# Four-row strips, later turns and a re-queued last layer in a two-layer attention and window-product kernel

## Chip, cores and metric

One core of one Trainium2 chip. The metric is device time of one execution in microseconds (us). The core has five engines that run their own instruction streams in order: TensorE (PE; its weight loads are listed as PEld), VectorE (DVE), ScalarE (ACT), GpSimd (POOL) and SyncE (SP). DMAs are issued by SyncE, ScalarE or GpSimd; what one engine has issued forms a queue of its own. In the profile q1 is SyncE's queue, q10 ScalarE's, and q0 (software_dynamic) GpSimd's.

## The reference, cut to what matters

The input x is one image of 48 channels, 256 x 256, in float32.

```python
# layer 0: x = x + L0(group_norm(x)), 16 groups
qkv = einsum('bchw,oc->bohw', xn, w_qkv)      # 48 -> 144 channels
qkv = dwconv3x3(qkv, w_dw)                     # depthwise, padding 1
q, k, v = (heads(unfold(t)) for t in split(qkv, 3))
# unfold: patches of 4x4 pixels, with a border of 4 zero pixels; 8 heads of 96 elements
attn = softmax(einsum('bhcn,bhcm->bhnm', l2norm(q), l2norm(k)) * temperature)
out = fold(einsum('bhcn,bhnm->bhcm', v, attn))
x = x + einsum('bchw,oc->bohw', out, w_proj)
# layer 1: x = x + L1(group_norm(x)); windows of 64x64 pixels
out = einsum('bcphqw,twW,thH,tcC->bCpHqW', xb, Ws, Hs, Cs)   # t = 3 terms
```

There are 4096 patches per head, so attention is 8 products of 4096 x 4096, with 96 elements per patch.

## The kernel before

The work runs in stages, and nearly all of the time is in the third.

**Start (0 to about 285 us).** Group sums of x, then the pointwise product to q, k and v for heads 0 and 1 (L154), written to a DRAM tensor t1[0]. The depthwise convolution of head 0 (class Depthwise, `depthwise_first`) follows; its patches go to DRAM as qkv[0].

**Attention (to about 3180 us).** For each of 8 heads h there are 16 groups g of 256 query rows; in each group two blocks of 128 rows. `scores` (L570) makes a block's 128 x 4096 scores in four PSUM tiles of the pool "big" (three buffers; matmuls at L344), and ScalarE takes their exponentials (L580). `weigh` (L606) multiplies the group's exponentials with the values (L614, three PSUM tiles of the same pool per group), and VectorE adds the result to an accumulator (L628). The order of every engine's instructions is the order in which the program text issues them (`tc.manual_schedule`). One group is written as: loads of values and keys, scores of two blocks, turns of values, then four steps k = 0 to 3, the first three with a `weigh` each.

Into this order the rest of layer 0 is woven:

- *Depthwise of the next head* (class Depthwise, L195): in groups 0 to 11 of heads 0 to 6, a row-block r is loaded in group r-1 (SyncE), gets its nine taps (VectorE, L232) in the next, and two groups after r is scaled, rearranged into patches (ScalarE, L286), split into a high and a low part (ScalarE L292, GpSimd L296) and stored from GpSimd (L302): the value patches as soon as they are there, the low part and both other stores at k=0. The low part's buffer is shared with the squares (L243) that VectorE reduces at L247.
- *Strips* (class Strip, L166): the pointwise product for heads 2 to 7 is made during head 0. A strip is two rows in each half of the image. Its steps are load (xs, SyncE L175), run (two matmuls at L181 into a "big" tile, then ScalarE's copy with bias into one of three buffers ot, L184) and store to t1[1] (two DMAs, SyncE L193). At steps k=1 and k=3 of each group two strips are run and two are loaded; at k=2 and at k=0 of the next group these two are stored. All 64 strips are done within head 0.
- *Values* (`load_value` L553, `turn` L559): a block of 512 values is loaded (vt, two buffers) and transposed on TensorE (L562) into vT (nine buffers). In head 0 the blocks 2 to 7 are loaded at the start of groups 1 to 6 and turned later in the same group. For the next head all eight are loaded and turned in groups 11 to 14, two a group. Group g needs block g // 2.

**Projection (about 3180 to 3337 us).** The attention's output comes back from DRAM (pot, L789), is multiplied with the projection (L803) and added to x (L810), group sums are taken (L814), and the result x1 is stored to DRAM (L819). After the last sums the statistics of layer 1 are worked out on small tiles; between them `occupy` (L840) issues matmuls whose result nobody reads: seven in a row ahead of the statistics, then single ones, all on the tile nmx.

**Last layer (from 3337 us).** Eight units u (a row of windows yw and one half xh of the width). `over_c` (L911) multiplies rows of x1 (pieces lxq in SBUF) with Cs into PSUM tiles pa, and the copy into zt (L933 on ScalarE for one in four, L935 on VectorE) turns the layout from rows outermost to rows innermost in memory. `over_w` (L940) multiplies with Ws and ScalarE copies the result (lyt, L956), `over_h` (L961) multiplies with Hs, and `residual` (L977) adds x1 rows (lrt) and stores the output from GpSimd. Per unit there are three thirds q, each with three `over_w`; the steps of `over_c` for the next unit are woven between them, so that twelve steps of unit 0 stand alone at the beginning. Loads of later rows and pieces are kept in a list, and `begin_load` (L906) issues one of them at a time from ScalarE.

Of the kernel before, what the change touches and what calls it, by code (L numbers as in the profile page):

```python
# [17 lines left out]
C = 48  # L18
# [21 lines left out]
NOT = 3  # L40
# [6 lines left out]
def conv_preact_kernel(  # L47
# [118 lines left out]
    class Strip:  # L166
# [5 lines left out]
        def load(self):  # L172
            self.xs = cv.tile([64 + C, 2, W], F32, name="xs", bufs=3)
            for s, rows in enumerate(both_halves(xc, 2 * self.j, 2)):
                nc.sync.dma_start(out=self.xs[s * 64 : s * 64 + C], in_=rows)  # L175

        def run(self, ps):
            self.ot = ots[self.j % len(ots)]
            for s in range(2):
                r = slice(s * 64, s * 64 + C)  # L180
                nc.tensor.matmul(  # L181
                    ps[:M1, s, :], lhsT=wr[r], rhs=self.xs[r].rearrange("p a b -> p (a b)"), start=True, stop=True
                )
            nc.scalar.activation(  # L184
                self.ot[:, :, 1 : W + 1],
                ps[:M1].rearrange("p s (a b) -> p (s a) b", a=2),
                AF.Identity,
                bias=bias[:M1, 1:2],
            )
# [305 lines left out]

    ots = [cv.tile([M1, 4, W + 2], F32, name=f"ot{i}") for i in range(NOT)]
    for t in ots:
        nc.gpsimd.memset(t[:, :, 0:1], 0.0)
        nc.gpsimd.memset(t[:, :, W + 1 : W + 2], 0.0)
    depthwise_first()  # L500

    with tc.If(nc.values_load(large) > 0):
        with tc.tile_pool(name="sps", bufs=2, space=PSUM) as sps:
            for j in range(HALF // 2):
                w = Strip(j)
                w.load()
                w.run(sps.tile([128, 2, 512], F32, name="sps"))
                w.store()
# [27 lines left out]
    with tc.tile_pool(name="ahead", bufs=2) as ah, tc.tile_pool(name="ae", bufs=3) as ae, tc.tile_pool(  # L536
# [3 lines left out]
        NS = 3  # L540
        RP = TP // PX * KS
# [17 lines left out]
        def turn(h, m):  # L559
# [3 lines left out]
            vT = ah.tile([128, 4, HD], F32, name="vT", bufs=9)  # L563
# [89 lines left out]
        strips = [[Strip(s)] if s < HALF // 2 else [] for s in range(NH * NG * NK + 2)]  # L653
        for s in range(2):
            for w in strips[s]:
                w.load()
        with tc.manual_schedule():
            load_query(0, 1)
            block = scores(0, 0)
            for h in range(NH):  # L660
                more = h + 1 < NH
                rows = {r: Depthwise(h + 1, r) for r in range(CR + 1)} if more else {}
                for g in range(NG):
# [45 lines left out]
                    if h == 0 and 0 < g <= 6:  # L709
                        turn(0, g + 1)  # L710
                    if more and CR + 2 <= g < CR + 6:
                        for m in range(2):
                            turn(h + 1, (g - CR - 2) * 2 + m)
                    if p:
# [7 lines left out]
                    for k in range(NK):  # L722
# [10 lines left out]
                        if s % 2:  # L733
                            for w in strips[s - 1] + strips[s]:
                                w.run(big.tile([128, 2, 512], F32, name="big"))
                            for w in strips[s + 1] + strips[s + 2]:
                                w.load()
# [40 lines left out]
    with tc.tile_pool(name="pj", bufs=3) as pj, tc.tile_pool(name="pjs", bufs=1) as pjs, tc.tile_pool(  # L778
# [61 lines left out]
        def occupy(n):  # L840

            for _ in range(n):
                nc.tensor.matmul(busy[:, 0:2, :], lhsT=ident[:, :P2], rhs=nmx, start=True, stop=True)
# [219 lines left out]
```

## Time and profile before

| what | us |
|---|---|
| three runs | 3591.67, 3596.32, 3598.53 (median 3596.32) |
| the profiled execution itself | 3602.95 |
| its span, first to last instruction | 3601.1 |
| busy: PE | 3365.5 |
| busy: DVE | 2026.6 |
| busy: ACT | 1911.9 |
| busy: POOL | 523.9 |
| head 0, groups 2 to 15 | 346.75 to 754.2 |
| one later head (head 1) | 348.8 |
| last layer's first product to its last | 3337.2 to 3593.2 |

The mean granted TensorE clock is 0.972 of full speed. A row of the profile's timeline gives start, duration, engine, line, operation, output <- inputs and the number of instructions merged in it; in square brackets stands the idle time of the engine just before, and what ended it. In the groups of instructions a row gives count, busy time, mean ns of one, then the idle time before. A fp32 matmul is recorded as two passes, so counts of L614, L181, L923, L949 and L968 are twice those of the program text; those of L344 are not.

### The profile page before, as it was taken

What the parts mean: (1) busy time and instruction counts of PE and PEld (TensorE: products, weight loads), DVE (VectorE), ACT (ScalarE), POOL (GpSimd) and SP (SyncE); (2) the same over time, 40 slices, a digit from 0 to 9 for tenths busy, and PEclk for the clock granted to TensorE, in tenths of its full rate; (3) what the DMA queues carried; (4) which work ended last, traced back from release to release, by engine and by line L of the source; (5) the groups of instructions that cost most, each with busy time, mean ns of one, the idle gap of its engine ahead of it and who ended that gap; (6) DMA issues with size and microseconds to landing.
All of it is one profiled execution on the core that took longest, in us unless ns stands there. A gap on an engine that the chain in (4) does not pass through costs nothing.

```text
span 3601.1 us, 63050 instructions
## 1 busy us (share of the span) xinstructions
PE 3365.5 (93%) x25842; PEld 1871.5 (52%) x25842; DVE 2026.6 (56%) x2983; ACT 1911.9 (53%) x2890; POOL 523.9 (15%) x584
## 2 busy tenths in 40 slices
PE   2878898999999999999999999999999999976898
PEld 1334444555555555555555555555555555532675
DVE  5463665148825882587268727862885222258454
ACT  0245666557655665576456646764666444410443
POOL 2030111012211220122012211221121100010001
PEclk9999999999999999999999999999999999986899
DMA  7455655543332333233333323332233221059664
GB/s 156 165 114 158 156 156 143 166 129 92 87 86 84 97 81 89 83 92 86 82 86 97 91 80 83 94 90 81 80 96 93 64 57 37 19 121 289 140 158 108
DMA packets 240271, 384.10 MB, mean 107 GB/s; under 512 B 77618, under 2 KB 175266, under 8 KB 235464
## 3 DMA queue, kind: packets, MB, share of 16 engines
q1 hardware_dynamic: 187974, 244.77, 24.3%
q0 software_dynamic: 33728, 106.40, 13.1%
q10 hardware_dynamic: 18274, 28.83, 3.6%
q8 instruction: 206, 3.38, 0.4%
q14 instruction: 89, 0.73, 0.1%
HBM read 234.76 MB, written 144.90 MB: 105 GB/s over the span
## 4 chain that ended last, share of the span: by engine, by line
PE 81%; DMA 6%; DVE 2%; issue 1%; ACT 1%; SPq 1%; ACTq 0%; POOL 0%; POOLq 0%; DVEq 0%
PE big L344 38%; PE big L614 36%; PE pc L968 2%; PE pa L923 2%; PE pb L949 2%; DMA t<-ot 1%; PE big L181 1%; DMA pot<-os__70 1%; DMA vt<-qkv 1%; DMA lxq<-x1s 1%; DVE lzt L935 1%; DMA pad<-t 1%; PE pst L562 1%; DVE xt L810 1%; DMA x1s<-pxt 0%
## 5 line engine op out<-in xcount | busy, mean ns | idle before, releaser
L580 ACT ACTIVATE e<-big,nmx 128x1024 f32<-128x1024 f32 x1024 | 1144.3, 1118 | 902.8 <-PE big L344 886.9
L344 PE MATMUL big<-kt,qt 128*128 128x512 f32 x6144 | 1460.2, 395 | 35.1 <-DMA kt<-qkv 26.8
L614 PE MATMUL big<-e,vn 128*32 128x512 f32 x12288 | 1353.7, 595 | 1.0 <-DVE vn L598 1.0
L344 PEld LDWEIGHTS big<-kt,qt 128*128 128x128 f32 x6144 | 1142.6, 189 | 377.4 <-issue 120.1
L628 DVE TENSOR_TENSOR oacc<-big,oacc 128x1024 f32<-128x1024 f32 x359 | 438.6, 1222 | 784.2 <-PE big L614 784.2
L614 PEld LDWEIGHTS big<-e,vn 128*32 128x32 f32 x12288 | 385.2, 110 | 888.3 <-issue 818.1
L232 DVE SCALAR_TENSOR_TENSOR acc<-pad,dwt,acc 126x1024 f32<-126x1024 f32 x592 | 765.6, 1293 | 33.8 <-DMA pad<-t 13.4
L302 POOL DMA_DIRECT2D qkv<-o x72 | 53.1, 737 | 1349.0 <-ACT o L286 1349.0
L296 POOL TENSOR_TENSOR ol<-o,oh 126x1024 fp32r<-126x1024 f32 x78 | 185.2, 2375 | 277.3 <-DVE ss L247 204.4
L594 DVE TENSOR_REDUCE zt<-zs 128x1 f32<-128x5 f32 x256 | 38.7, 151 | 329.8 <-ACT e L580 329.8
L580 ACT ACTIVATION_READ_ACCUMULATOR e<-big,nmx 128x1 f32 x1024 | 196.4, 192 | 0.0
L286 ACT COPY o<-acc 126x1024 f32<-126x1024 f32 x74 | 160.7, 2172 | 0.0
L184 ACT ACTIVATE ot<-big,bias 108x1024 f32<-108x1024 f32 x64 | 68.9, 1112 | 136.7 <-PE big L181 71.0
L935 DVE COPY lzt<-pa 128x864 f32<-128x864 f32 (+1 forms) x69 | 102.1, 1525 | 63.5 <-PE pa L923 63.5
L956 ACT COPY lyt<-pb 128x1024 f32<-128x1024 f32 x69 | 70.9, 1028 | 112.6 <-PE pb L949 106.3
L803 PE MATMUL pps<-pot,wp 96*96 96x512 f32 x128 | 77.8, 773 | 53.3 <-DMA pot<-os__70 40.2
L213 ACT ACTIVATE acc<-pad,dwt 126x1024 f32<-126x1024 f32 x74 | 84.0, 1135 | 73.5 <-DMA pad<-t 73.5
L221 PE MATMUL dps<-pad,diag 126*126 126x512 f32 x216 | 96.4, 606 | 15.0 <-DMA pad<-t 15.0
L243 ACT ACTIVATE sq<-acc 126x1024 f32<-126x1024 f32 x74 | 78.4, 1060 | 59.8 <-DVE acc L232 48.9
L147 ACT ACT_TABLE_LOAD x2 | 2.6, 1283 | 202.6 <-DMA x1s<-pxt 149.2
L247 DVE TENSOR_REDUCE ss<-sq 126x64 f32<-126x1024 f32 x80 | 97.4, 1218 | 6.7 <-ACT sq L243 6.7
L949 PE MATMUL pb<-wsb,lzt 64*64 64x64 f32 x4608 | 88.8, 223 | 11.4 <-issue 7.2
(138 smaller groups left out, 1901.2 us busy)
## 6 DMA issues: line engine op xcount, KB each, us to landing
pad<-t SPq DMA_DIRECT2D x238, 254.0 KB
t<-ot SPq DMA_DIRECT2D x128, 217.7 KB
qkv<-ol POOLq DMA_DIRECT2D x78, 336.0 KB, 6.4
qkv<-oh POOLq DMA_DIRECT2D x70, 336.0 KB, 5.6
qt<-qkv SPq DMA_DIRECT2D x176, 96.0 KB
xs<-in_x_dram SPq DMA_DIRECT2D x128, 96.0 KB
pot<-os__70 SPq DMA_DIRECT2D x16, 768.0 KB
qkv<-o POOLq DMA_DIRECT2D x72, 168.0 KB, 3.4
```

What stands on the lines that cost most here:

```text
L213: nc.scalar.mul(self.acc, self.pad[:, 0:KS, 0:W], dwt[:, self.h, 0:1])
L221: nc.tensor.matmul(ps[:, i, :], lhsT=diag[:, tap, :], rhs=self.pad[:, y : y + 2, dx : dx + W], start=(tap == 0), stop=(tap == 8),)
L232: nc.vector.scalar_tensor_tensor(self.acc, self.pad[:, dy : dy + KS, dx : dx + W], dwt[:, self.h, tap : tap + 1], self.acc, ALU.mult, ALU.add,
L247: nc.vector.tensor_reduce(self.ss, self.sq.rearrange("p a (x b) -> p x a b", b=KS), AX.XY, ALU.add)
L286: nc.scalar.copy(self.o.rearrange("p (a b) x -> p a b x", a=KS), self.acc.rearrange("p a (x b) -> p a b x", b=KS))
L296: eng.tensor_sub(self.ol, self.o, self.oh.bitcast(F32))
L344: nc.tensor.matmul(ps[:, i, :], lhsT=qt[:, r, q0 : q0 + 128], rhs=kts[2 * j + i][:, r // 2, :], start=(r == 0), stop=(r == 2),)
L580: nc.scalar.activation(e[:, j * 1024 : (j + 1) * 1024], ps.rearrange("p a b -> p (a b)"), AF.Exp, bias=nmx[:, b : b + 1], accum_out=zs[:, ...
L614: nc.tensor.matmul(ps[p * 32 : (p + 1) * 32, u, :], lhsT=vn[:, c * 32 : (c + 1) * 32], rhs=e[:, n * 512 : (n + 1) * 512], start=(i == 0), ...
L628: nc.vector.tensor_add(oaccs[h, pair], ps, old)
L935: nc.vector.tensor_copy(to, src)
L949: nc.tensor.matmul(pb[s * WS : (s + 1) * WS, w, n * WS : (n + 1) * WS], lhsT=zts[u][r, t * C + b * 24 + q * 8 + s * 4 + i, :], rhs=wsb[r, ...
```

## The change

Four things are changed together.

1. Strips have four rows instead of two (`SR = 4`), so there are 32, with two buffers ot and two buffers xs of double size. One strip is run at k=1 and one at k=3, each in two parts of two matmuls and one copy; the next is loaded right after. The strip of k=1 is stored at k=2 and that of k=3 at k=0 of the next group, now from GpSimd, behind the depthwise's low part and stores at k=0.
2. Values: in head 0 the blocks 2 to 7 are loaded in groups 1, 2, 4, 5, 7 and 8 and turned two groups after that. For later heads seven blocks are loaded and turned in groups 11 to 14 of the head before, and the eighth is loaded in group 1 and turned in group 2 of its own head. vT has eight buffers.
3. Last layer: each load is issued from SyncE. Ahead of it SyncE issues a store of one element of the tile that was just copied, to a small DRAM tensor `turns`, so that the load is issued after that copy has been made. The copies of `over_c` keep input, output and engine but run with rows innermost.
4. The seven idle products ahead of the statistics become four, which read the last additions' result and the group sums.

```diff
-NOT = 3
+NOT = 2
+SR = 4
...
-            self.xs = cv.tile([64 + C, 2, W], F32, name="xs", bufs=3)
+            self.xs = cv.tile([64 + C, SR, W], F32, name="xs", bufs=2)
...
+            for i in range(0, SR, 2):
+                ps = pool.tile([128, 2, 512], F32, name="big")
...
+                nc.scalar.activation(
+                    self.ot[:, :, i : i + 2, 1 : W + 1],
...
         def store(self):
-            for s, rows in enumerate(both_halves(t1[1], 2 * self.j, 2, base=1)):
-                nc.sync.dma_start(out=rows, in_=self.ot[:, 2 * s : 2 * s + 2, :])
+            for s, rows in enumerate(both_halves(t1[1], SR * self.j, SR, base=1)):
+                nc.gpsimd.dma_start(out=rows, in_=self.ot[:, s])
...
-            vT = ah.tile([128, 4, HD], F32, name="vT", bufs=9)
+            vT = ah.tile([128, 4, HD], F32, name="vT", bufs=8)
...
+        LOADS = (1, 2, 4, 5, 7, 8)
...
-                    if h == 0 and 0 < g <= 6:
-                        load_value(0, g + 1)
+                    if h == 0 and g in LOADS:
+                        load_value(0, 2 + LOADS.index(g))
                     if more and CR + 2 <= g < CR + 6:
-                        for m in range(2):
+                        for m in range(2 if g < CR + 5 else 1):
                             load_value(h + 1, (g - CR - 2) * 2 + m)
+                    if h > 0 and g == 1:
+                        load_value(h, NM - 1)
...
-                    if h == 0 and 0 < g <= 6:
-                        turn(0, g + 1)
+                    if h == 0 and g - 2 in LOADS:
+                        turn(0, 2 + LOADS.index(g - 2))
...
+                    if h > 0 and g == 2:
+                        turn(h, NM - 1)
...
                         if k == 0 and p:
                             p.low(nc.gpsimd)
                             p.store((0, 1))
-                        if s % 2:
-                            for w in strips[s - 1] + strips[s]:
-                                w.run(big.tile([128, 2, 512], F32, name="big"))
-                            for w in strips[s + 1] + strips[s + 2]:
-                                w.load()
-                        elif s:
-                            for w in strips[s - 2] + strips[s - 1]:
-                                w.store()
+                        if s % 2 and s // 2 < len(strips):
+                            strips[s // 2].run(big)
+                            if s // 2 + 1 < len(strips):
+                                strips[s // 2 + 1].load()
+                        elif s % 2 == 0 and 0 < s // 2 <= len(strips):
+                            strips[s // 2 - 1].store()
...
-            occupy(7)
-            mv1, e1 = group_stats(st1, mean1, rstd1, pjs, pp1, lambda: occupy(1))
+            for ki in range(0, KS, 2):
+                occupy(xt[:, ys.start + ki : ys.stop : KS, :])
+            for i in range(0, 4, 2):
+                occupy(st1[:, : HALF * W // 512 - 3 + i, :])
+            mv1, e1 = group_stats(st1, mean1, rstd1, pjs, pp1, lambda: occupy(nmx))
...
-                        loads.append(lambda s=s, c=c: load_rows(yw, q, s, c, 4, nc.scalar))
+                        loads.append(lambda s=s, c=c: load_rows(yw, q, s, c, 4, nc.sync))
...
-        def begin_load():
-
-            if loads:
+        def begin_load(behind):
+
+            if loads and behind is not None:
+                n = len(taken)
+                taken.append(nc.sync.dma_start(out=turns[:, n : n + 1], in_=behind))
                 loads.pop(0)()
...
-                    if (p * 3 + g) % (4 if u else 2) == 1:
-                        nc.scalar.copy(to, src)
-                    else:
-                        nc.vector.tensor_copy(to, src)
+                    copy = nc.scalar.copy if (p * 3 + g) % (4 if u else 2) == 1 else nc.vector.tensor_copy
+                    copy(to.rearrange("p s y k -> p s k y"), src.rearrange("p s y k -> p s k y"))
...
-                    yield
+                    yield zt[0:1, 0, y : y + 1]
...
-                        begin_load()
+                        begin_load(parts[u, q][0:1, t, 0:1])
                         if t < 2:
                             for _ in range(2):
-                                next(ahead, None)
-                                begin_load()
+                                begin_load(next(ahead, None))
```

In the changed kernel the lines from L173 on are numbered some 1 to 15 higher.

More of the change, by code (lines that the diff above doesn't have):

```diff
@@ L494, in conv_preact_kernel @@
     one = attention.enter_context(tc.tile_pool(name="one", bufs=2, space=PSUM))
[L496 removed]
+    ots = [cv.tile([M1, 2, SR, W + 2], F32, name=f"ot{i}") for i in range(NOT)]
     for t in ots:
[L498 to L499 removed]
+        nc.gpsimd.memset(t[:, :, :, 0:1], 0.0)
+        nc.gpsimd.memset(t[:, :, :, W + 1 : W + 2], 0.0)
     depthwise_first()
@@ L503, in conv_preact_kernel @@
         with tc.tile_pool(name="sps", bufs=2, space=PSUM) as sps:
-            for j in range(HALF // 2):
+            for j in range(HALF // SR):
                 w = Strip(j)
                 w.load()
-                w.run(sps.tile([128, 2, 512], F32, name="sps"))
+                w.run(sps)
                 w.store()
@@ L647, in conv_preact_kernel @@
             turn(0, m)
-        strips = [[Strip(s)] if s < HALF // 2 else [] for s in range(NH * NG * NK + 2)]
-        for s in range(2):
-            for w in strips[s]:
-                w.load()
+        strips = [Strip(j) for j in range(HALF // SR)]
+        strips[0].load()
         with tc.manual_schedule():
@@ L889, in conv_preact_kernel @@
         loads = []
+        turns = dram.tile([1, 256], F32, name="turns")
+        taken = []
         def rows_later(yw, q):
```

43 lines of the change are left out of this document (23 added, 20 removed).

## The prediction

> **What bounds the kernel now.** I read the table of windows first, because the page's sums mix stages; then TensorE's timeline where the table shows it idle, then the engine named there. Columns of the windows: length, busy time of PE, PEld, DVE, ACT, POOL, granted clock, DMA share, GB/s.
>
> ```profile
> 346.75:647.60 300.85, 272.08 (x1643) 138.02 (x1641) 183.26 (x281) 191.01 (x262) 50.46 (x40) 0.95 0.58 152
> 647.60:754.20 106.60, 106.60 (x666) 56.62 (x665) 19.05 (x36) 58.83 (x94) 7.08 (x13) 0.97 0.58 170
> 754.20:1103.00 348.80, 348.80 (x2350) 196.39 (x2352) 219.91 (x341) 216.88 (x339) 57.75 (x53) 1.00 0.35 89
> 3337.00:3360.00 23.00, 19.20 (x153) 16.27 (x156) 8.72 (x6) 8.71 (x6) 0.00 (x0) 0.50 0.30 55
> 3360.00:3594.00 234.00, 214.06 (x6068) 160.50 (x6060) 125.92 (x90) 100.36 (x90) 19.55 (x28) 0.98 0.60 141
> ```
>
> Row 3 is head 1: PE is never idle, at full clock; the other heads look alike. Nothing that the change does there can show. Row 1 is groups 2 to 11 of head 0 (the strips run here): 29 us idle and a lower clock. Rows 4 and 5 are the last layer: its first 23 us run at half clock, then 20 us idle. Between head 7 and the last layer (3177 to 3337) the DMA share is near 1.0, and the change moves no transfer there. So the change can act in head 0 and in the last layer alone.
>
> What stops PE in head 0 (its timeline; in brackets the idle time before a row, and who ended it):
>
> ```profile
> 385.76 0.58 PE L562 MATMUL pst<-ident,vt 96*128 96x96 f32 x4 [3.11 <-DMA vt<-qkv]
> 386.26 8.77 PE L614 MATMUL big<-e,vn 128*32 128x512 f32 x64
> ...
> 406.98 8.50 PE L344 MATMUL big<-kt,qt 128*128 128x512 f32 x36 [1.40 <-ACT ot L184]
> ...
> 586.85 3.90 PE L181 MATMUL big<-xs,wr 48*108 48x512 f32 x8 [10.76 <-DMA xs<-in_x_dram]
> ```
>
> Three waits: a turn for a value block loaded in the same group, scores for ScalarE's copy into ot (itself waiting for an older store), strips for their load, late in SyncE's queue. Each costs twice: after 3.11 us idle the 64 products take 8.77 us and not 7.07. An undisturbed group lasts 25.75 us (scores from 528.06 to 553.81). Ten would be 257.5, with 2.3 us of turns 260; they took 300.85. **Excess 41 us**; in row 2 another 3 (a group at 647.6 that began cold). So 44 us is there to be had.
>
> **The change, part by part.**
>
> *Strips and turns: what goes.* The turns come two groups after their load; the wait of L562 (11.6 us, five times, on PE) goes. Loads and stores of a strip halve in number (128 to 64 each), and the stores leave SyncE's queue, so xs comes in time. In heads 1 to 7 one value block of eight is turned in group 2 of its own head, loaded a group earlier: no added wait, and head 1 has no idle time to give. I take all 44 us as removed.
>
> *Strips: the wait that is added.* There are two ot buffers instead of three. The strip of step k=3 writes the second one in each group; its store is issued at k=0 of the next group, and the buffer is written again at k=3 of that group. On POOL this store stands behind the patch store, the subtraction L296, and two 336 KB stores (L302), in groups 2 to 11. In the undisturbed group:
>
> ```profile
> 545.50 2.36 POOL L296 TENSOR_TENSOR ol<-o,oh 126x1024 fp32r<-126x1024 f32 x1 [3.29 <-DVE ss L247]
> 547.81 0.98 POOL L302 DMA_DIRECT2D qkv<-oh  x1
> 548.75 1.06 POOL L302 DMA_DIRECT2D qkv<-ol  x1
> ```
>
> and the queue's own rows (packets, MB, share; then count, KB, us from issue to landing, head 2's window):
>
> ```profile
> q0 software_dynamic: 33728, 106.40, 13.1%
> qkv<-ol POOLq DMA_DIRECT2D x10, 336.0 KB, 6.2
> ```
>
> Step by step: ol is issued at 548.75 and lands 6.2 us later, 554.95. Behind it come 2 x 435 KB. q0 moves 106.4 MB in 13.1% of 3601 us, 225 GB/s while it works, so 870 KB take 3.9 us: 558.85. Only then may ScalarE copy the strip (base: 551.45, 1.12 us each). Behind that copy on ScalarE stand the next exponentials; on PE the next scores, because strips and scores share three "big" buffers and the one needed is freed by that copy. So scores go on at 558.85 + 1.1 = 560.0, not at 553.81: 6.2 us. To it comes the cold start (after 4.34 us idle a row of 7.07 took 9.25): about 2. From it goes what VectorE gains in the idle time, since the sum before L296 ends earlier: about 1.5. I take **7 us** a group. Group 11 has no reduction ahead of L296 (in the trace it starts 4 us sooner): 3 us. 9 x 7 + 3 = **66 us**. Bounds: 3 us a group if the strip stores overlap the ol store to its last microsecond (30 us in all); above, the rows of ol in head 0 itself land after 11.2 us, but beside stores that leave SyncE, so I take 10 a group (93).
>
> The Trainium skill, "DMA: Bandwidth & Descriptors", section "Issuing engine by pattern", would have plain stores issued from SyncE. Its section on one DMA gives about 2 us plus bytes over 436 GB/s; the two stores by themselves would be an estimated 4 us, which leaves the place in the queue as the cost.
>
> Head 0 in all: 66 - 44 = **+22** (from -14 to +49).
>
> *Last layer, copies with rows innermost.* The copies write 4-byte pieces 256 bytes apart today. Rows by form:
>
> ```profile
> L935 DVE COPY lzt<-pa 128x864 f32<-128x864 f32 x46 | 77.4, 1707 | 48.0 <-PE pa L923 48.0
> L628 DVE TENSOR_TENSOR oacc<-big,oacc 128x1024 f32<-128x1024 f32 x359 | 438.6, 1222 | 784.2 <-PE big L614 784.2
> L286 ACT COPY o<-acc 126x1024 f32<-126x1024 f32 x74 | 160.7, 2172 | 0.0
> L286 ACT COPY o<-dps 126x1024 f32<-126x1024 f32 x6 | 6.1, 1012 | 13.6 <-DVE dps L281 10.3 <-issue 3.3
> ```
>
> 1707 ns for 864 elements against 1222 for 1024 contiguous ones: nearly double. L286 tells where strides cost: read from SBUF in steps of 16 bytes 2172, from PSUM 1012. So a write in runs of three (12 bytes) may cost 1.05 to 1.7 us; I take 1.2, nearest to L247, which reads runs of four at full rate (1218 for 1024). The read now steps 576 bytes through PSUM; no row shows VectorE doing that.
>
> The rule against it: "SBUF — State Buffer", section "Door 1: The DMA port swizzle", gives SBUF lines of 16 bytes, which agrees with the rows above, but PSUM lines of 8 bytes, outside of which access is slow for matmuls. If that held for these copies they would stay at 1.7 us, and with no gain from copies the sum at the end of this part would be +13 instead of +9.
>
> In the first 22 us of the layer (3337.2 to 3359.35) PE's own work at half clock is 8 x 1.89 + 4 x 1.36 = 20.6 us. With copies out of the way 1.5 us are saved; if unbroken work lets the clock rise as it did 6.5 us after 586.85, about 16 us remain and 6 are saved. I take -4.
>
> *Last layer, loads from SyncE.* Today they sit on ScalarE between its copies:
>
> ```profile
> 3529.62 3.47 ACTq L884 DMA_DIRECT2D lrt<-x1s  x2
> 3533.14 1.60 ACT L933 COPY lzt<-pa 128x864 f32<-128x864 f32 x1 [2.66 <-DMA lrt<-x1s]
> ```
>
> Two issues hold the copy for 2.66 us, and PE waits 1.96 behind it. Of the 20 us idle some 5 lie in the last 25 us, where no load is left. The steps that are long by PE's third product (10.6, 10.4, 11.2, 12.8 us against 9.1 to 9.5) add to 8. With shorter copies I take -9; bounds 0 and -17. The small stores on SyncE (88, one per load) wait for a copy's end; behind them only loads are queued, which the consumers need several steps later. SyncE has no other work here; an issue on it takes 0.3 to 0.6 us. If the loads came late for every second step, 1 us each would cost 12: upper bound +3 for the sum.
>
> *Idle products.* Before, 14 rows run from 3325.5 to 3330.5 in one go; now four, held back by the additions and sums they read, fill about the same time, beside VectorE's last additions, which set the end. Cost 0. If they kept the clock at 1.0 into 3337 they would save up to 8; if one came late, +1.
>
> Last layer in all: **-13** (from +4 to -25). Sum: +22 - 13 = **+9 us** on the profiled execution's own 3602.95 us (its span 3601.1). That run was 6.6 us above the median of the runs, so I put the change on the median: 3596.3 + 9 = **3605**.
>
> **Rivals.**
>
> 1. *Faster: the store lands early enough.* The point is 4.4 us a group: below it, head 0 gets shorter. At 3 us a group (30 in all) head 0 gains 14; with the 13 of the last layer the time is 3569. For: large packets, and SyncE's queue nearly empty of stores. Against: POOL's order puts them behind two stores that need 6.2 us even in head 2.
> 2. *The last layer gives little* (copies stay at 1.7 us, clock stays at half): -3, with the 22 of head 0, 3615. For: no row of such a read on VectorE, and the clock stayed at 0.5 at 83% busy. Against: L286 from PSUM.
> 3. *The store wait is larger*: 10 us a group, 93 in all, +49 - 13, 3632. For: ol lands after 11.2 us in head 0 today. Against: over a third of that traffic (8 x 218 KB of 152 GB/s x 30.1 us a group) was SyncE's own stores.
>
> **Chances.** A measurement of this kernel tells about 0.2% (7 us) from no change. Forecast 0.42 (3595 to 3615: 0.22 slower, 0.20 within), rival 1 0.36 (0.33 faster, 0.03 within), rival 2 0.13 and rival 3 0.09, both slower. Faster 0.33, within 0.2% 0.23, slower 0.44. Range: down to 3566 to take in most of rival 1, up to 3630 for half of rival 3.
>
> **What would show it.** In the profile after: POOL's stores t<-ot behind L302, ScalarE's copy into ot waiting for DMA t<-ot once a group in groups 2 to 11, PE idle 4 to 6 us after six score products, groups of about 32.5 us there and 25.8 in groups 12 to 15; no wait of pst for vt, none of strips for xs. In the last layer: lzt copies near 1.2 us on both engines, no DMA issue on ScalarE, a clock above 0.5 before 3355, PE idle below 12 us of the rest. Wrong if the ot copies do not wait (rival 1), or if the copies keep 1.7 us (rival 2).

## The result, and the profile after

The changed kernel takes **3652.4 us** (median of four runs, 3635.4 to 3658.8) against 3597.4 for the kernel before: ratio 1.0146, 95% interval 1.0108 to 1.0184, some 55 us slower. The forecast was 3605, its range ended at 3630. Single executions that ran far longer than all others of their kernel (6750 us in e4, 15546 in f4, one of 15132 of the kernel before) are slow runs and left out of every median and ratio here. The profiled execution took 3658.8 us, with a span of 3657.0 (before: 3601.1).

The table of windows after, cut as before: ten groups of head 0, the rest of head 0, head 1, the last layer's first steps, its rest to the last product. Columns as before: length, busy time of PE, PEld, DVE, ACT, POOL, granted clock, DMA share, GB/s.

```profile
346.69:700.78 354.09, 281.74 (x1654) 151.39 (x1652) 184.59 (x281) 191.37 (x264) 72.64 (x80) 0.89 0.48 128
700.78:805.30 104.52, 104.52 (x655) 54.88 (x656) 19.05 (x36) 57.73 (x93) 14.90 (x27) 0.98 0.56 161
805.30:1154.10 348.80, 348.80 (x2348) 196.45 (x2352) 219.81 (x340) 217.22 (x339) 59.92 (x58) 1.00 0.35 91
3397.00:3414.50 17.50, 14.82 (x132) 13.07 (x132) 5.91 (x6) 5.24 (x6) 0.00 (x0) 0.64 0.39 73
3414.50:3650.00 235.50, 214.09 (x6080) 162.90 (x6080) 94.17 (x90) 88.94 (x90) 19.50 (x28) 0.97 0.60 140
```

Row 1 is the loss: 354.1 us for ten groups that took 300.9. PE is idle for 72 us of them, and its clock fell from 0.95 to 0.89. Row 3 is head 1, unchanged to a tenth. Row 4 is shorter than before (17.5 against 22.1), row 5 is not. From the starts of the first score, the first score of head 1, the last score, the projection's first and last product and the last layer's first products, the 56 us of the two profiles are:

| stretch | before | after | difference |
|---|---|---|---|
| start to first score | 274.5 | 273.2 | -1.3 |
| head 0 | 459.8 | 512.1 | +52.3 |
| heads 1 to 7 | 2448.3 | 2448.8 | +0.5 |
| to the projection's first product | 27.7 | 28.3 | +0.6 |
| projection's products | 114.7 | 123.1 | +8.4 |
| statistics | 12.1 | 11.5 | -0.6 |
| last layer, first steps | 22.1 | 17.5 | -4.6 |
| last layer, rest to the end | 241.8 | 242.6 | +0.8 |

PE's timeline after, where it stood idle before it (three of ten such rows; the other seven are alike, 5.0 to 8.1 us):

```profile
485.00 12.28 PE L351 MATMUL big<-kt,qt 128*128 128x512 f32 x42 [8.12 <-ACT ot L191]
521.81 12.63 PE L351 MATMUL big<-kt,qt 128*128 128x512 f32 x42 [8.05 <-ACT ot L191]
559.37 12.61 PE L351 MATMUL big<-kt,qt 128*128 128x512 f32 x42 [8.45 <-ACT ot L191]
```

No wait for vt and none for xs is left in head 0. In their place stands one wait ahead of each group from 3 to 12, and 42 score products that took 9.80 us now take 11.4 to 12.6 behind it. What ends it, in the timeline of POOL and ACT in one group:

```profile
541.50 2.35 POOL L303 TENSOR_TENSOR ol<-o,oh 126x1024 fp32r<-126x1024 f32 x1 [2.30 <-DVE ss L254]
542.89 2.12 ACT L191 ACTIVATE ot<-big,bias 108x1024 f32<-108x1024 f32 x2 [1.69 <-PE big L184]
543.80 1.00 POOL L309 DMA_DIRECT2D qkv<-oh  x1
544.77 1.04 POOL L309 DMA_DIRECT2D qkv<-ol  x1
545.68 2.27 POOL L200 DMA_DIRECT2D t<-ot  x4
558.21 2.12 ACT L191 ACTIVATE ot<-big,bias 108x1024 f32<-108x1024 f32 x2 [13.19 <-DMA t<-ot]
```

POOL comes to the strip's store only at 545.68, when the strip of k=1 has been copied too, so all four stores leave at once. The copy of the strip of k=3 (last row) waits 13.2 us for the first two of them. The issues that start in this window (size of one, then us from issue to landing; SyncE's loads have none):

```profile
t<-ot POOLq DMA_DIRECT2D x4, 435.4 KB, 12.1
xs<-in_x_dram SPq DMA_DIRECT2D x2, 192.0 KB
qkv<-oh POOLq DMA_DIRECT2D x1, 336.0 KB, 7.0
qkv<-ol POOLq DMA_DIRECT2D x1, 336.0 KB, 11.0
vt<-qkv SPq DMA_DIRECT2D x1, 192.0 KB
```

The last layer's rest, groups of instructions from 3414 us on (busy, mean ns, then idle time before and who ended it):

```profile
L964 PE MATMUL pb<-wsb,lzt 64*64 64x64 f32 x4608 | 89.1, 223 | 14.0 <-issue 11.6 <-ACT lyt L971 1.6 <-ACT lzt L950 0.7
L983 PE MATMUL pc<-lyt,hsb 64*64 64x512 f32 x576 | 74.3, 626 | 6.8 <-issue 5.5 <-DVE lrt L997 1.3
L950 DVE COPY lzt<-pa 128x864 f32<-128x864 f32 (+1 forms) x63 | 61.5, 1002 | 56.0 <-PE pa L940 56.0
L950 ACT COPY lzt<-pa 128x864 f32<-128x864 f32 (+1 forms) x22 | 20.1, 914 | 13.0 <-PE pa L940 13.0
```

The same products in the kernel before, from 3359 us on:

```profile
L949 PE MATMUL pb<-wsb,lzt 64*64 64x64 f32 x4608 | 88.8, 223 | 11.4 <-issue 7.2 <-ACT lyt L956 2.4 <-ACT lzt L933 1.2
L923 PE MATMUL pa<-csn,lxq 49*128 49x144 f32 x896 | 70.7, 300 | 6.4 <-ACT lzt L933 2.6 <-DVE lzt L935 2.5 <-issue 0.9
L968 PE MATMUL pc<-lyt,hsb 64*64 64x512 f32 x576 | 70.3, 601 | 2.6 <-DVE lrt L982 1.3 <-issue 1.3
```

The copies are as fast as hoped: 1002 and 914 ns in the mean, 1531 and 1568 before. PE waits 2.3 us for the copies into lzt and lyt, where it waited 8.7. But its idle time put down to "issue", time for which the profile shows no releaser, is 17.6 us with the 0.5 of L940; before it was 9.4 in the same stretch. It lies inside runs of equal products whose inputs are all there. Below it is called idle time without a releaser.

### The profile page after: what moved, and what is told of

It is laid out like the page before. It is cut to its first block, busy times and chain, and to the rows that moved or that the text cites. A ratio compares the mean times of both kernels' runs of the same rounds, so it can differ in the third digit from the quotient of the medians.

```text
span 3657.0 us, 63059 instructions
## 1 busy us (share of the span) xinstructions
PE 3369.8 (92%) x25836; PEld 1882.6 (51%) x25836; DVE 1992.7 (54%) x2983; ACT 1896.7 (52%) x2890; POOL 558.5 (15%) x646
## 5 line engine op out<-in xcount | busy, mean ns | idle before, releaser
L351 PE MATMUL big<-kt,qt 128*128 128x512 f32 x6144 | 1477.8, 398 | 104.1 <-ACT ot L191 72.3
L351 PEld LDWEIGHTS big<-kt,qt 128*128 128x128 f32 x6144 | 1156.8, 191 | 449.4 <-issue 116.3
L303 POOL TENSOR_TENSOR ol<-o,oh 126x1024 fp32r<-126x1024 f32 x78 | 185.2, 2375 | 265.9 <-DVE ss L254 192.7
L950 DVE COPY lzt<-pa 128x864 f32<-128x864 f32 (+1 forms) x69 | 67.4, 1000 | 67.4 <-PE pa L940 67.4
```

The lines of the kernel that those rows point to most:

```text
L303: eng.tensor_sub(self.ol, self.o, self.oh.bitcast(F32))
L351: nc.tensor.matmul(ps[:, i, :], lhsT=qt[:, r, q0 : q0 + 128], rhs=kts[2 * j + i][:, r // 2, :], start=(r == 0), stop=(r == 2),)
```

## The experiments

Times are medians; ratios are to the kernel before, on the same chip (its medians there were 3592.8 to 3599.1 us). "Head 0", "first steps" and "rest" are stretches of the table above, each read from one profiled execution.

### Head 0: the place of the store in GpSimd's order

**e1_strip_store_first**, the changed kernel with two statements swapped:

```diff
-                        if k == 0 and p:
-                            p.low(nc.gpsimd)
-                            p.store((0, 1))
                         if s % 2 and s // 2 < len(strips):
...
                         elif s % 2 == 0 and 0 < s // 2 <= len(strips):
                             strips[s // 2 - 1].store()
+                        if k == 0 and p:
+                            p.low(nc.gpsimd)
+                            p.store((0, 1))
```

> The changed kernel, but at k=0 the strip's store is issued on GpSimd ahead of the low part L303 and the stores of oh and ol, not behind them. Theory (place in the queue): the copy into ot at k=3 waits only because its buffer's store stands behind L303, oh and ol; issued at k=0 itself it has some 18 us to land and lands in 12. The ten waits of PE on ot (5 to 8.5 us each, with a slow restart 9.9 us a group) go, groups 2 to 12 of head 0 take 25.8 to 26.5 us, head 0 is shortened by some 95 us and the time is 3652 - 95 = 3557. Rival (too few buffers): with two buffers the store of 870 KB beside the other stores is late wherever it is issued, or the wait passes to the buffer of k=1, whose store at k=2 now stands behind oh and ol, or to the buffers of oh and ol; some 5 us a group remain, 50 in all, and the time is about 3605.

Measured: 3554.8, ratio 0.9889 (0.9848 to 0.9930). Head 0 takes 415.6 us, 96.5 less than in the changed kernel; all groups from 2 on take 25.5 to 26.9, by the starts of their scores. One group in its timeline:

```profile
489.08 1.09 POOL L200 DMA_DIRECT2D t<-ot  x2
491.92 2.36 POOL L303 TENSOR_TENSOR ol<-o,oh 126x1024 fp32r<-126x1024 f32 x1 [1.75 <-DVE ss L254]
494.23 1.00 POOL L309 DMA_DIRECT2D qkv<-oh  x1
495.23 1.05 POOL L309 DMA_DIRECT2D qkv<-ol  x1
498.87 2.12 ACT L191 ACTIVATE ot<-big,bias 108x1024 f32<-108x1024 f32 x2 [3.98 <-DMA t<-ot]
500.60 9.81 PE L351 MATMUL big<-kt,qt 128*128 128x512 f32 x42
```

The store leaves 2.8 us ahead of L303. ScalarE still waits 4 us for it, but that is in time for PE: the 42 products have no idle time before them and take 9.81 us. Two buffers are enough; the order was the cost, and it cost more than the whole change lost.

**e11_store_after_low**, the store between L303 and the stores of oh and ol:

```diff
                             p.low(nc.gpsimd)
+                            if 0 < s // 2 <= len(strips):
+                                strips[s // 2 - 1].store()
                             p.store((0, 1))
```

> The changed kernel, but at k=0 the strip's store is issued between the low part L303 and the stores of oh and ol: it waits for L303 as before, but no longer stands behind these 672 KB. Theory (the two stores ahead of it and what shares the DMA engines with them are the cost): issued 1.9 us earlier and first in the queue, the store lands some 6 us earlier than in the changed kernel (12 us after its issue there); of the 9.9 us a group at most 3 are left, head 0 takes 420 to 445 us and the time is 3555 to 3585. Rival (L303's late start is the cost, since it waits for VectorE's sum 17 us into the group): the copy into ot still waits some 5 us a group, head 0 takes 465 us or more, the time is 3605.

Measured: 3577.3, ratio 0.9944 (0.9925 to 0.9963); head 0 takes 435.1 us.

```profile
481.13 2.36 POOL L303 TENSOR_TENSOR ol<-o,oh 126x1024 fp32r<-126x1024 f32 x1 [2.29 <-DVE ss L254]
483.43 1.12 POOL L200 DMA_DIRECT2D t<-ot  x2
490.11 2.12 ACT L191 ACTIVATE ot<-big,bias 108x1024 f32<-108x1024 f32 x2 [5.48 <-DMA t<-ot]
491.27 3.03 PE L351 MATMUL big<-kt,qt 128*128 128x512 f32 x12 [0.73 <-ACT ot L191]
```

Now the copy starts 6.7 us after the store's issue begins, not 12.5. So of the 96.5 us between the changed kernel and e1, 77 (512.1 - 435.1) come from standing behind oh and ol, and 19.5 (435.1 - 415.6) from waiting for L303. The three profiled executions lie up to 10 us from their medians; the medians of the times give 75 and 22.5.

**e2_strip_store_sync**, `nc.gpsimd.dma_start` of the strips made `nc.sync.dma_start`:

> The changed kernel, but the strips are stored from SyncE instead of GpSimd, at the same places of the program text. Theory (place in the queue): SyncE has nothing that holds the store for long, so the ten waits on ot go; the loads of xs stand behind these stores again and one or two come late, as in the kernel before (10.8 us once), so 85 of the 99 us of head 0 come back and the time is about 3567. Rival (too few buffers, or the DMA engines themselves too busy at that point): the copy still waits some 5 us a group, 3605.

Measured: 3568.5, ratio 0.9938 (0.9914 to 0.9962). No wait on ot is left; strips wait for xs five times, 0.5 to 1.9 us each, and head 0 takes 425.2 us (in an execution 10 us below the median). The store needs an order in which nothing holds it. GpSimd is one such place, SyncE nearly as good another. The Trainium skill, "DMA: Bandwidth & Descriptors", section "Issuing engine by pattern", gives plain stores to SyncE; here the first place on GpSimd was by the medians 14 us faster than SyncE (the intervals overlap), and the place behind the other stores some 80 us slower.

### Head 0: the turns

**e4_turns_only**, the kernel before with the value blocks loaded in groups 1, 2, 4, 5, 7, 8 and turned two groups later (and eight buffers vT):

> The kernel before, with nothing changed but the values: in head 0 loaded in groups 1, 2, 4, 5, 7, 8 and turned two groups later, the eighth block of later heads in their own head, eight buffers. Theory: the five waits of PE for vt (11.6 us) go and with each the slow products behind it (1.2 to 2.2 us), some 20 us, and nothing is added in heads 1 to 7: 3577. Rival: the two stalls that follow in the same groups (scores for the copy into ot, 1.4 to 2.5 us, and strips for xs) grow by what the turns no longer hold back, since the strips' stores and loads are late on SyncE's queue all the same: at most 8 us gained, 3589.

Measured: 3592.0, ratio 0.9994 (0.9974 to 1.0014): nothing. Its profile shows 439.4 us for head 0, 20 less than in the kernel before, but that execution was 13 us below the median, and in e3, which leaves head 0 as it was, head 0 took 452.8. No turn waits there; strips and scores do:

```profile
397.36 8.49 PE L344 MATMUL big<-kt,qt 128*128 128x512 f32 x36 [0.91 <-ACT ot L184]
423.13 1.25 PE L181 MATMUL big<-xs,wr 48*108 48x512 f32 x2 [4.48 <-DMA xs<-in_x_dram]
489.04 9.91 PE L344 MATMUL big<-kt,qt 128*128 128x512 f32 x36 [2.86 <-ACT ot L184]
546.27 10.08 PE L344 MATMUL big<-kt,qt 128*128 128x512 f32 x36 [3.63 <-ACT ot L184]
```

**e9_turns_early** is the reverse: e1 with head 0's loads and turns where they were before.

> The kernel with the strip's store first, but in head 0 the value blocks are loaded in groups 1 to 6 and turned in the same group, as before. Theory (each edit of head 0 removes its own waits): the five waits for vt come back, 11.6 us with 8 us of slow products behind them, the time is 3555 + 20 = 3575. Rival (vt was late only because the strips' stores stood ahead of it on SyncE's queue): with these on GpSimd the blocks land in time, and the time stays at 3555 to 3560.

Measured: 3559.1, ratio 0.9902 (0.9870 to 0.9933), with no wait for vt in its profile and 415.4 us for head 0. So once strips have four rows and their stores leave GpSimd in time, the place of the turns is worth nothing: vt is there without it. Before the change it was worth nothing either (e4). Which part of the strips' change ended the three waits is less clear. Stores in SyncE's queue alone don't bring them on: in e2 they are still there, with half as many transfers of twice the size and the later turns, and only the short waits for xs are left. Nor do these stores hold SyncE long in the kernel before: there its loads of xs wait longer, for the products of an older strip (waits of SyncE from 330 to 700 us: total, times, longest):

```profile
SPq L175 <- PE big L181: 43.0, 15, 5.8
SPq L193 <- ACT ot L184: 5.0, 20, 0.3
```

Strips of two rows stored from GpSimd, which would tell size from queue, were not run.

### Last layer: copies, loads and PE's own instructions

**e3_copies_only**, the kernel before with the copies' two operands rearranged and nothing else:

> The kernel before, with nothing changed but the copies of over_c, which run with rows innermost; loads stay on ScalarE, one after a copy. Theory (the loads from SyncE cost what the copies gain): copies take 1.0 us instead of 1.5 to 1.7, the first steps of the last layer take 17.5 us instead of 22.1, and in the remaining 242 us the waits of PE for copies (some 10 us) go while the idle time inside a run of products that waits for nothing shown stays at the 9 us of the kernel before, so the layer is 12 us shorter: 3585. Rival (PE meets its own instruction supply as soon as copies no longer hold it): that idle time grows to 17 us without any load on SyncE, and only the 4.6 us of the first steps are gained: 3593.

Measured: 3590.9, ratio 0.9983 (0.9963 to 1.0003). First steps 18.8 us (also with the old idle products), rest 244.8; the idle time of PE without a releaser rose from 9.4 to 15.8 with loads still on ScalarE. By the profile this is the rival; the interval of the time alone would also hold the theory's 3585.

**e8_loads_scalar**, e1 with `nc.scalar` for the late loads and without the small stores; **e10_no_turns**, e1 with the loads on SyncE and without the small stores:

```diff
-            if loads and behind is not None:
-                n = len(taken)
-                taken.append(nc.sync.dma_start(out=turns[:, n : n + 1], in_=behind))
+            if loads:
                 loads.pop(0)()
```

> The kernel with the strip's store first, but the last layer's loads are issued from ScalarE again, without the small stores and their DRAM tensor; copies stay with rows innermost. Theory (the move to SyncE is worth only ScalarE's waits, some 3 us, since PE's instruction supply sets the pace): ACT's copies wait for issues again, the rest of the last layer takes 240 to 245 us instead of 235 to 243, the time 3558. Rival (the loads from SyncE bunch and delay PE's instructions): idle time for nothing shown falls from 15 to 10 us, the rest to 234, the time to 3550. Besides, the stage of the projection took 118.6 to 123.1 us in three kernels with the small DRAM tensor and 113.6 to 116.8 in three without it: if the tensor is the reason, this run shows at most 117 there.

> The kernel with the strip's store first, but SyncE issues the last layer's loads without the small stores ahead of them, so each waits only for the tile that it overwrites. Theory (the turns only spread loads that no one waits for): SyncE has little to hold, loads are issued somewhat earlier, the time stays within 4 us of 3555. Rival (loads in a bunch fill the DMA engines and PE's instructions come later): idle time for nothing shown grows from 15 to 25 us, the time to 3565. If the small DRAM tensor makes the projection's stage longer, that stage falls to 117 us here.

Measured: 3563.7 (0.9915, 0.9882 to 0.9948) and 3575.0 (0.9949, 0.9926 to 0.9971), against 3554.8 with SyncE and small stores. In e8 the rest takes 244.2 us with 21.0 of idle time without a releaser: the theory's rest, and neither side's idle time. In e10 the rest takes 257.2 us with 24.0 of idle time without a releaser, and the clock in the first 60 us of it is 0.89. Its SyncE, its PE in one place, and the queues from 3419 to 3434 us (packets, MB, share of the 16 DMA engines' time):

```profile
3387.41 27.55 SPq L784 DMA_DIRECT2D lxq<-x1s  x16
3415.13 10.61 SPq L897 DMA_DIRECT2D lrt<-x1s  x12
```

```profile
3425.11 1.02 PE L979 MATMUL pc<-lyt,hsb 64*64 64x512 f32 x3
3431.08 3.69 PE L979 MATMUL pc<-lyt,hsb 64*64 64x512 f32 x16 [4.95 <-issue]
```

```profile
q1 hardware_dynamic: 2945, 2.83, 100.1%
q8 instruction: 2, 0.03, 1.1%
```

Without its turns SyncE issues 12 to 16 loads in a row. They fill all 16 DMA engines, and between the two instruction packets of these 15 us and the one just ahead of them lie up to 9.4 us, where one comes every 5 us in the mean (47 in the 242 us of the layer's rest before, though with one distance of 9.7 there too). PE stops for 4.95 us after the first three of a run of equal products. So by the medians the small stores are what makes the move to SyncE pay: against ScalarE, 6 to 9 us less with them (f1 below and e1, the same kernel; the intervals overlap), 11 more without. The Trainium skill, "DMA: Bandwidth & Descriptors", section "Issuing engines are not separate DMA queues", says that all issuers' transfers run on the same 16 engines and that spreading the issue saves only the issuers' time; in this window q1 and q8 do share them (100.1% and 1.1%). The runs add that instructions are among what shares them, and that which engine issues, and behind what, was worth more here than its own time.

**e7_no_late_loads**, e1 with the rows and pieces of the first units used again, no load behind them:

> The kernel with the strip's store first (as in e1_strip_store_first), but the last layer loads nothing after its first rows and pieces: later units read the rows and pieces that are already there, so some 23 of 34 MB that move in the last 240 us are left out (the result is then not that of the reference). Theory (PE's instructions come late because they share the DMA engines with these loads): PE's idle time inside runs of products, put down to nothing shown (12.5 to 17.6 us with fast copies, about 48 instruction packets of 16 KB), falls below 4 us, the rest of the last layer takes 226 us instead of 235 to 243, and the time is 3543. Rival (an instruction packet takes its time whatever else moves): the idle time stays at 12 to 17 us, the rest at 235 or more, the time at 3555.

Measured: 3548.0 (0.9866, 0.9832 to 0.9900), between the two. The rest takes 230.2 us, and 9.7 of the idle time stay. Loads are a part of it, not the whole.

That this idle time is a wait for instructions can be read from the packets of queue q8, 16 KB each. They come in step with PE's instructions: 47 in the rest of the last layer before, for 12178 products and weight loads, and 19 for 4673 from 760 to 1100 us in head 1, some 250 each. In the 18 profiles PE's rest of the last layer has 166 idle times of 0.5 us or more without a releaser, and every one ends 1.2 to 1.8 us after such a packet is in; the 4.95 us above end at 3431.08, after a packet that was in at 3429.76. They hold all but 0.2 to 2 us of the idle time of this kind in each profile, e7 too. What makes a packet come late when no load is in its way is not shown.

**e12_slow_copies** (e1 with the old copies and old idle products), **e13_small_loads** (e1 with lrt loads of two channels, not four) and **e14_small_loads_slow_copies** (e13 with the old copies):

> The kernel with the strip's store first, but over_c's copies write as before, and the seven idle products ahead of the statistics are those of before: of the last layer's changes only the loads from SyncE are left. Theory (copies and PE's instruction supply hide each other): copies take 1.5 to 1.7 us again, the first steps 22.1 us, the idle time for nothing shown falls to 8 to 10 us as in the kernel before, ScalarE's copies no longer wait behind loads (3 us less than before), so the rest takes 238 us as against 234 to 243; time 3559. Rival (the copies are worth what was forecast, 9 us in the rest of the layer): rest 245, time 3566. If the idle products made the projection's stage longer (118 to 123 us in seven kernels that have the new ones, 114 to 117 in three that have the old ones), it takes 117 us or less here.

> The kernel with the strip's store first, but the last layer's loads of x1 rows (lrt, 256 KB in packets of 1 KB) are cut into halves, each behind its own small store, so that the same bytes come in shorter bursts. Theory (bursts of loads hold PE's instructions back): idle time for nothing shown falls from 12 to 15 us to 8 to 10, the rest of the layer from 237 to 231 us, the time from 3555 to 3550. Rival (PE's instructions come as late behind short bursts as behind long ones, or the loads now come too late for their consumers): no gain, 3555 to 3562.

> The kernel of e13_small_loads (strip's store first, last layer's loads in halves from SyncE), with over_c's copies writing as before. Theory (copies and PE's instruction supply hide each other, so the copies are worth only their 4 us in the first steps, where PE stands for little else): first steps 22.1 us instead of 18.6, the rest 226 to 232 us as with the fast copies (227.8), time 3551 + 3 = 3554. Rival (with loads in short bursts PE's instructions are on time, so PE waits for copies again and they are worth what was forecast): the rest takes 236 us or more, the time 3563.

Measured: 3553.2 (0.9873, 0.9848 to 0.9898), 3550.9 (0.9866, 0.9838 to 0.9893) and 3559.0 (0.9900, 0.9882 to 0.9917), so with large loads the copies seem worth nothing, with small ones something. The rests are 232.9, 227.8 and 238.0 us, with 7.9, 11.0 and 9.4 of idle time without a releaser. As e14 ran on another chip, the four were measured again side by side:

> The kernel with the strip's store first: large loads, copies with rows innermost (as e1_strip_store_first), now beside the three others on one chip. Theory (PE's instruction supply takes up what the copies gain while loads are large): within 4 us of f2, 3555. Rival (the copies are worth 9 to 13 us as forecast, and the earlier comparison was chance): 9 us or more faster than f2.

> As f1_large_fast, with the copies (and the idle products) of the kernel before. Theory: within 4 us of f1, 3554. Rival: 9 us or more slower than f1, 3564.

> As f1_large_fast, with the loads of x1 rows cut into halves. Theory (shorter bursts let PE's instructions come earlier): 4 to 8 us faster than f1, 3549, and with them the copies pay, so 6 to 10 us faster than f4. Rival (the size of a load does nothing): within 3 us of f1.

> As f3_small_fast, with the copies of the kernel before. Theory: 6 to 10 us slower than f3, 3557. Rival (the supply takes up the copies' gain here too, and the earlier difference was between chips): within 4 us of f3.

| kernel | us | ratio (interval) | first steps | rest | idle without a releaser |
|---|---|---|---|---|---|
| f1, large loads, new copies | 3557.8 | 0.9905 (0.9882 to 0.9928) | 19.1 | 239.1 | 15.4 |
| f2, large loads, old copies | 3557.2 | 0.9902 (0.9881 to 0.9923) | 22.2 | 235.1 | 7.6 |
| f3, small loads, new copies | 3547.7 | 0.9880 (0.9855 to 0.9905) | 17.4 | 230.2 | 9.3 |
| f4, small loads, old copies | 3556.5 | 0.9904 (0.9881 to 0.9928) | 22.1 | 235.7 | 11.4 |

PE's products in the rest of f1, then of f3:

```profile
L964 PE MATMUL pb<-wsb,lzt 64*64 64x64 f32 x4608 | 88.1, 223 | 10.5 <-issue 8.1 <-ACT lyt L971 1.6 <-ACT lzt L950 0.7
L983 PE MATMUL pc<-lyt,hsb 64*64 64x512 f32 x576 | 73.2, 618 | 7.0 <-issue 5.6 <-DVE lrt L997 1.3
```

```profile
L964 PE MATMUL pb<-wsb,lzt 64*64 64x64 f32 x4608 | 87.8, 222 | 9.7 <-issue 7.4 <-ACT lyt L971 1.6 <-ACT lzt L950 0.7
L983 PE MATMUL pc<-lyt,hsb 64*64 64x512 f32 x576 | 71.2, 605 | 3.0 <-issue 1.6 <-DVE lrt L997 1.3
```

(f2 also has the old idle products; the first steps, 22.2 beside 22.1 in f4 with the new ones, show nothing of them.) With loads of 256 KB the copies' gain is given back as idle time without a releaser (7.6 to 15.4), and the sum is nil; with loads of 128 KB it stays, 9 us by the medians (8 between e13 and e14). The intervals of f3 and the other three overlap, so this is not a sure size. f3 is the fastest kernel: 1.2% below the kernel before and, on other chips, 105 us below the changed one by the medians.

A rest is read from one execution, and executions differ. The changed kernel, e1, e2, e9, e11 and f1 have the same last layer, and its rest took 242.6, 237.2, 234.9, 234.0, 230.9 and 239.1 us, with 11.8 to 17.6 of idle time without a releaser. With the old copies and these loads it took 232.9 and 235.1 (e12, f2), with small loads and new copies 227.8 and 230.2 (e13, f3), and with loads from ScalarE 241.8 and 241.4 before and in e4, 244.8 and 244.2 with the new copies (e3, e8). By these profiles, what the rest gained came from the loads behind small stores; without the smaller loads the new copies brought it nothing.

## Why the prediction was wrong

**The mechanism of head 0 was right, its size was not.** The chain was as told: POOL's store behind L303, oh and ol, ScalarE's copy behind the store, the next scores behind the copy. The step that failed is "7 us" a group. Its terms, with what the ten waits of the changed kernel show:

- The wait, put at 6.2 us, was 7.2 in the mean (5.0 to 8.45). The step "ol lands 6.2 us later" took a landing time from head 2, and "behind it come 2 x 435 KB" left out that POOL, coming late, issues the two stores of k=1 with them. In this window ol took 11.0 and the strip's store 12.1: oh, ol, four strip stores, two loads of xs and one of vt, 3.0 MB, are issued within 4.2 us. The prediction had the 11.2 us of ol in head 0 before it and set it aside, because "over a third of that traffic" was SyncE's stores. Those left SyncE, but not the window.
- The cold start was put at 2 and was 1.6 to 2.8.
- "From it goes what VectorE gains in the idle time, about 1.5" did not happen: L303 starts 18.1 to 19.7 us after the 42 scores do in groups 3 to 10 (541.50 - 521.81), where it was 17.4 in the group without idle time; the slow scores moved VectorE's sum back.
- Group 11 was put at 3 us; its wait, the one ahead of group 12, was 5.0.

354.1 us for ten groups is 94 over the 260 of undisturbed ones, where the prediction had 66. Less the 41 that left, that is +53 in row 1. Rival 3 had this case, 93 for head 0, at a chance of 0.09.

**The 44 us to be had were there**, and e1 shows them: 415.6 against 459.8. (In e3, with head 0 as before, it was 452.8, so another execution gives 37.) But the text gave the turns their own share of it. e4 and e9 show that they have none: the waits went with the strips.

**Last layer: the first steps came out, in part by luck; the rest failed.** -4 was foretold and -4.6 came, but the sum had 1.5 of it from the copies and the rest from a clock that rises in unbroken work. It did not rise: the granted clock was 1.0 in the first 4.8 us of these steps and 0.5 to their end (0.64 in the mean). In e1, e9 and f1, at 0.50 throughout, they took 19.1 us, against 22.1 to 22.2 with the old copies at 0.50. So 3.0 us are the copies' and 1.6 the clock's, and the clock at the start differed between executions (17.4 to 19.1 us with the same last layer). The row that the prediction took the rise from was misread as well: after 586.85 the granted clock rose at 595.21, 8.4 us later and not 6.5. The copies came to 1125 ns (VectorE) and 1028 (ScalarE) for 864 elements, where 1.2 us was taken, and the waits that the prediction counted went. What it had not asked is what PE meets next. The step that failed is "With shorter copies I take -9": it became +0.8 in the profiled execution, since PE's idle time without a releaser, waits for instructions, grew by 8.2 us. That execution is the longest of the six with this last layer; their mean is 236.5, some 5 us less than before, still not 9, and by e12 and f2 the loads brought it, not the copies. Before, 9.4 us of the 20 idle were already of that kind, which the groups of instructions showed; the prediction counted the other kind and let all of it be gain. It also left out that loads would share the DMA engines with instructions. (Its +13 for copies that gain nothing does not follow from its terms: that leaves -9 for the last layer, where its own rival 2 leaves -3, with the clock at half besides.)

**Not foreseen, not settled:** "So the change can act in head 0 and in the last layer alone" left out the projection, whose products took 8.4 us longer. The stage varies: 113.6 to 116.8 us in three profiles with strips of two rows, 117.3 to 123.1 in fifteen with strips of four (117.3 and 121.8 for one and the same kernel). In all of them the DMA share is 1.0 and 31 to 32 MB move, so what differs is the rate, 274 GB/s before and 259 after. The small DRAM tensor isn't the reason (120.9 and 117.8 without it), nor are the idle products (120.4 and 120.8 with the old ones). Whether the strips are, and how, was not tried; the cause stays open.

**The sum:** of the 47 us between 3605 and 3652, head 0 holds 30 (52.3 against 22), the last layer 9 (-4.6 + 0.8 against -13) and the projection 8 in the profiled execution.

## What to carry to other kernels

When a store is moved to another queue, write down what stands ahead of it there at that moment and when its buffer is needed again; one swap of two statements was worth over 90 us here. Take a transfer's landing time from the same window, with all that starts in the same few microseconds, not from a quieter one. When a wait is removed, look first at the idle time that has no releaser: it may take over what the removed wait gave. And read a stage's gain of a few microseconds from several executions: six of one last layer differed by 12 us.

## What the runs showed of the hardware

- PE's instructions travel with the data, in packets of 16 KB for some 250 products and weight loads, and all 166 longer idle times without a releaser in the last layer's rest end 1.2 to 1.8 us after a packet is in. With loads in a row at a DMA share of 1.0, 9.4 us lay between two packets, and PE stopped for 4.95 us in mid-run (e10). By which rule the DMA engines pass the packets on is not shown.
- A copy on VectorE that reads PSUM in steps of 576 bytes and writes runs of three elements took 1125 ns for 864 elements, 1.30 ns each; contiguous additions took 1222 for 1024, 1.19 each. Writing 4-byte pieces 256 bytes apart took 1707, 1.98 each. Nearly all of the cost was the write's stride, not the read's. The rule that the prediction weighed against the change ("SBUF — State Buffer", section "Door 1: The DMA port swizzle", with lines of 8 bytes in PSUM) is told there for matmuls; on these copies it does not show: the prediction had them at 1.7 us if it held, and they took 1125 ns.
